# Attention and a 16-entry look-up FFN on one core: look-ups of 1024 columns, placed by two running counts, and six down blocks kept in DRAM

## Chip, cores, metric

One NeuronCore of a Trainium2 chip runs the whole program. The metric is the device time of one execution in microseconds; the median of three runs of the kernel before is 1066.1 us (1065.95 to 1067.05). The engines are named as in the profile: PE (TensorE, matmul), PEld (its weight loads), DVE (VectorE), ACT (ScalarE), POOL (GpSimd) and SP (SyncE, which here only issues DMAs).

## What is computed

All in float32; x has shape (2, 2048, 512), the hidden size of the FFN is 1376, and each FFN weight is an entry of a table of 16.

```python
def attn(x, Wq, Wk, Wv, Wo):          # attention over the 512 features, not over tokens
    q, k, v = x @ Wq, x @ Wk, x @ Wv
    s = softmax(q.T @ k / 4, axis=-1) # 512 x 512, one per batch entry
    return (s @ v.T).T @ Wo
def ffn(x, lut, gate_idx, up_idx, down_idx):
    h = silu(x @ lut[gate_idx].T) * (x @ lut[up_idx].T)   # 1376 wide
    return h @ lut[down_idx].T
x = x + attn(layernorm(x), ...)
x = x + ffn(layernorm(x), ...)
```

## The kernel before, in words

The 4096 tokens are eight chunks of 512. The attention is folded into one 512 x 512 matrix for each batch entry, which is multiplied with the normalized chunks ("y products", 175 to 290 us). The FFN's gate and up products follow (290 to 750 us), then the last 96 of the 1376 hidden rows ("rows", 750 to 798), then the down products in two halves (798 to 931, and 931 to the end).

**Products with fewer multiplications.** Gate, up and down products are done on 2 x 2 blocks with seven products in place of eight (Strassen-Winograd): each needs sums of weight blocks and of activation blocks, named S1 to S4 and T1 to T4, and folds the seven results together. Hidden rows are taken in blocks f of 128 (f = 0 to 10, the last has 96), tokens in pairs p of chunks (p = 0 to 3). A *unit* is one (f, p). From f=2 on, some block products take part in a second level over f and f+1 and over p and p+1: the `Second` objects of_b, of_c and of_d hold sums over both f (tiles lb, lc, ld, made by `sums_left`) and activation sums that are kept in DRAM and loaded again. A unit's role 0 to 3 says where it stands in that square of four. Unit (f, 1) with f even has role 1: right after its first product a1 it multiplies with S2 of lc (`extra0`). Units with f odd take partial results back from DRAM by POOL's DMAs (`add_part` into p1 and u2, `back` into y).

**Order by hand.** The program order of PE, ACT, DVE and SP is the order in which the Python code emits instructions; POOL's queue is ordered by the framework. Each engine works off its queue in order. `Line.run` emits the stages of a unit (a1, c1, a2, c2, b, a3, a4 of the unit before) and calls `between()` after most of them.

**Weights by look-up.** A `Job` makes 512 columns of one weight block (gate, up or down) from int32 indices: `fetch` loads the indices, `cast` (ACT) makes an int16 copy, and `ops` (a generator, all on DVE) makes three masks of single bits and one full-word mask, eight leaves (each chooses between two table entries) and seven merges with copy_predicated. Each `yield` gives the estimated cost of the step emitted. The tiles: `idx` two buffers, results `wg` and `wu` three each. The gate job of block f may start when f < 3 + passed (units of f-3 emitted), the up job when f < 3 + ended (the last a4 of f-3 emitted, one unit later). After an up job, `of_both` makes the sums S1 to S4 of the block (four DVE operations on 256 columns).

`pump(us)` emits look-up steps worth `us`. In gate/up, `between()` first loads or does one thing from a list (sums_left when ready, otherwise one of `todo`), and pumps 0.3 after an operation of `todo`, nothing after sums_left, and `pace[0]` (0.6 to 1.4 by role, 0.75 in down) otherwise. Before a unit, a loop makes sure that its weights are there, and before p = 1 those of f+1 and the lc, lb, ld sums: it emits all steps that are still missing at once.

```python
        while f not in gu or f > 1 and p and not all(o.ready(f | 1) for o in seconds):
            step()
        ...
        while p and sums_of:
            next_sums_left()
```

Down blocks: eleven, of 128 hidden rows x 512. Blocks 0 to 5 lie in `wd`, a tile that is held in SBUF from the start; 6 to 10 are looked up during the first half of down. `down_sums` makes the T sums of the pairs of blocks; `Hidden` loads h from DRAM by SP's queue and makes its S sums, listed in `todo`. The class `LastRows` copies (ACT, lines 1250 and 1251) and sums the weights of block 10; it is set up after the last unit.

Of the kernel before, what the change touches and what calls it, by code (L numbers as in the profile page):

```python
# [62 lines left out]
P = 128  # L63
# [6 lines left out]
def tile_attn_ffn(  # L70
# [39 lines left out]
    wdp = ctx.enter_context(tc.tile_pool(name="wdp", bufs=1))  # L110
# [8 lines left out]
    wd = wdp.tile([P, K1, E], F32, tag="wd", name="wd")  # L119
# [18 lines left out]

    def sub(dest, a, b):
        nc.vector.tensor_tensor(dest, a, b, ALU.subtract)  # L140

    def add(dest, a, b):
        nc.vector.tensor_tensor(dest, a, b, ALU.add)  # L143
# [102 lines left out]
    class Job:  # L246
        def __init__(self, name, rows, cols, load, dest, after, gate):
            self.name, self.rows, self.cols = name, rows, cols
            self.load, self.dest, self.after, self.gate = load, dest, after, gate

        def fetch(self, queue=nc.gpsimd):
            self.idx = gub.tile([P, 512], I32, tag="idx", name=f"idx_{self.name}", bufs=2)[
                : self.rows, : self.cols
            ]
            self.load(queue, self.idx)

        def cast(self):
            self.b3 = self.bits("b3", 2)
            nc.scalar.copy(self.b3, self.idx)

        def bits(self, tag, bufs):
            t = gub.tile([P, 512], I16, tag=tag, name=f"{tag}_{self.name}", bufs=bufs)
            return t[: self.rows, : self.cols]

        def ops(self):

            rows, f, idx, b3 = self.rows, self.cols / 1024, self.idx, self.b3
            vec = nc.vector
            w = self.dest()
            b1, b2 = self.bits("b1", 1), self.bits("b2", 1)  # L270
            vec.tensor_scalar(b1, b3, 2, None, ALU.bitwise_and)
            vec.tensor_scalar(b2, b3, 4, None, ALU.bitwise_and)
            yield 0.2 + 0.54 * f

            vec.tensor_scalar(idx, idx, 31, 31, ALU.logical_shift_left, ALU.arith_shift_right)
            yield 0.1 + 0.55 * f
            vec.tensor_scalar(b3, b3, 8, None, ALU.bitwise_and)
            yield 0.1 + 0.27 * f
            masks = [None, b1, b2, b3]

            def pick(level, at, dest):

                if level == 1:
                    k = at // 2
                    vec.tensor_scalar(  # L285
                        dest.bitcast(I32), idx, lut_x[:rows, k : k + 1],
                        lut_i[:rows, at : at + 1], ALU.bitwise_and, ALU.bitwise_xor,
                    )
                    yield 0.2 + 0.55 * f
                    return  # L290
                yield from pick(level - 1, at, dest)
                half = 1 << (level - 1)
                t = gub.tile(
                    [P, 512], F32, tag="pick", name=f"{self.name}_{level}_{at}", bufs=3
                )[:rows, : self.cols]
                yield from pick(level - 1, at + half, t)
                vec.copy_predicated(dest, masks[level - 1], t)  # L297
                yield 0.1 + 1.17 * f

            yield from pick(4, 0, w)  # L300
            yield from self.after()

# [6 lines left out]
    def gate_job(f):  # L309
        f0, rows = FT[f]  # L310
        n = KB * rows

        def load(queue, idx):
            queue.dma_start(idx, gate_idx[:, KB * f0 : KB * f0 + n])

        def dest():
            t = wgu.tile([P, KB, P], F32, tag="wg", name=f"wg_{f}", bufs=3)
            gw[f] = t.rearrange("p k r -> p (k r)")[:, :n]
            return gw[f]

        def after():
            gw[f] = gw[f].rearrange("p (k r) -> p k r", k=KB)
            yield 0.1

        return Job(f"g{f}", P, n, load, dest, after, lambda: f < 3 + passed[0])

    def up_job(f):
        f0, rows = FT[f]
        n = KB * rows
        up = []  # L330

        def load(queue, idx):
            queue.dma_start(idx, up_idx[:, KB * f0 : KB * f0 + n])

        def dest():
            t = wgu.tile([P, KB, P], F32, tag="wu", name=f"wu_{f}", bufs=3)
            up.append(t.rearrange("p k r -> p (k r)")[:, :n])
            return up[0]

        def after():  # L340
            uw[f] = up[0].rearrange("p (k r) -> p k r", k=KB)
# [4 lines left out]
        def of_both():  # L346
# [4 lines left out]
            for op, d, v, w in (  # L351
                (add, s1, a21, a22), (sub, s2, s1, a11), (sub, a21, a11, a21), (sub, s4, a12, s2)
            ):
                op(d, v, w)
                yield 0.42
            gu[f] = {"11": a11, "12": a12, "S3": a21, "22": a22, "S1": s1, "S2": s2, "S4": s4}

        return Job(f"u{f}", P, n, load, dest, after, lambda: f < 3 + ended[0])

    def down_job(i):  # L360
        f0, rows = FT[i]
        return Job(
            f"wd{i}", rows, E, lambda queue, idx: queue.dma_start(idx, down_idx[f0 : f0 + rows, :]),
            lambda: wd_block(i)[:rows], lambda: iter(()), lambda: i < K1 or wd2,
        )

    wd2 = []

    def wd_block(i):
        return wd[:, i, :] if i < K1 else wd2[0][:, i - K1, :]  # L370


    jobs = [job(f) for f in range(2) for job in (gate_job, up_job)]
    jobs += [down_job(i) for i in range(4)]
    for f in range(2, NFT - 1, 2):
        jobs += [gate_job(f), up_job(f), gate_job(f + 1), up_job(f + 1)]
        jobs += [down_job(i) for i in {6: (4,), 8: (5,)}.get(f, ())]
    jobs += [gate_job(NFT - 1), up_job(NFT - 1), *(down_job(i) for i in range(K1, NFT))]
    assert len(jobs) == 3 * NFT

    def looked_up():

        for i, job in enumerate(jobs):
            while not job.gate():
                yield None
            if i == 0:
                job.cast()
            for k, cost in enumerate(job.ops()):
                yield cost
                if k == 9 and i + 1 < len(jobs):  # L390
                    jobs[i + 1].cast()
            if i + 2 < len(jobs):
                jobs[i + 2].fetch()
# [4 lines left out]
    def step():  # L398
# [6 lines left out]
        return next(lookup, None)  # L405

# [20 lines left out]
    jobs[1].fetch(nc.sync)  # L427
# [337 lines left out]
    def turn(to, t):  # L765

        nc.vector.transpose(to.rearrange("p m (t b) -> p m t b", b=Q), t)
# [124 lines left out]
    class Second:  # L892
# [32 lines left out]
        def ready(self, f):  # L925
            return f in gu if self is of_d else f in gw and len(gw[f].shape) == 3 and f in uw
# [78 lines left out]
    def mm(ps, pairs, first):  # L1005

        for i, (lhsT, rhs) in enumerate(pairs):
            nc.tensor.matmul(  # L1008
# [4 lines left out]
    class GateUp:  # L1013
# [52 lines left out]
        def c2(self):  # L1066
            if self.role is None:
                mm(self.c, self.pairs("22", "T4"), False)
                add(self.u2, self.c, self.u2)
            elif self.role == 0:  # L1070
                of_c.begin(self, "11", "11")
                mm(self.c, of_c.pair(self, "12", "21"), False)
                add(self.u2, of_c.ps, self.u2)
                add(self.u2, self.c, self.u2)
            elif self.role == 1:
                add(self.u2, self.c, self.u2)
                of_c.go_on(self, "S4", "22")
                add(self.u2, of_c.ps, self.u2)
# [30 lines left out]
        def b(self):  # L1109
# [3 lines left out]
            elif self.role == 0:  # L1113
# [3 lines left out]
                add(h0, self.p1, h0)  # L1117
            elif self.role == 1:
                of_b.go_on(self, "S4", "22")
                add(h0, of_b.ps, self.p1)  # L1120
            elif self.role == 2:
                of_b.go_on(self, "22", "T4")
                add(h0, of_b.ps, self.p1)
# [8 lines left out]
        def a3(self):  # L1132
            mm(self.a, self.pairs("S1", "T1"), False)
            self.c22 = self.temp("c22")
            add(self.c22, self.a, self.p7)

        def first(self):
            if self.role == 2:
                add(self.u2, of_c.ps, self.u2)
            if self.role in (2, 3):  # L1140
                add(self.u2, self.c, self.u2)
            nc.vector.tensor_tensor(self.h0, self.h0, self.u2, ALU.mult)
            self.store(self.h0, 2 * self.p)

        def a4(self):
# [3 lines left out]
            elif self.role == 0:  # L1149
# [3 lines left out]
                add(h1, self.a, h1)  # L1153
            elif self.role == 1:
                of_d.go_on(self, "S4", "22")
                nc.scalar.copy(h1, of_d.ps)
                add(h1, self.a, h1)
            else:
                if self.role == 2:
                    mm(self.a, of_d.pair(self, "22", "T4"), False)  # L1160
                    add(self.y, of_d.ps, self.y)
                add(h1, self.a, self.y)
# [6 lines left out]
        def out(self):  # L1169
            nc.vector.tensor_tensor(self.h1, self.h1, self.c22, ALU.mult)  # L1170
            self.store(self.h1, 2 * self.p + 1)

    class Line:
# [5 lines left out]
        def run(self, u, final=False):  # L1179
# [24 lines left out]
            self.between()  # L1204
            if role == 3:
                last_a4()
            u.extra2()
# [24 lines left out]
    class LastRows:  # L1232
# [5 lines left out]
        def __init__(self):  # L1238
            s = [wgu.tile([P, 3, 2, P], F32, tag="s", name=f"last_{i}", bufs=2) for i in range(2)]
            flat = [  # L1240
                t.rearrange("p a b c -> p (a b c)").rearrange("p (k r) -> p k r", k=KB) for t in s
            ]
            self.w, self.v = flat
            t = last_pool.tile([P, KB, 2 * LAST], F32, tag="last", name="last_2")
            self.u = t

        def weights(self):
            f, r = NFT - 1, LAST
            w, v, u = self.w, self.v, self.u
            nc.scalar.copy(w[:, :, :r], gw[f])  # L1250
            nc.scalar.copy(w[:, :, r:], uw[f])  # L1251
# [54 lines left out]
    pace = [1.0]  # L1306
# [4 lines left out]
    def between():  # L1311
# [4 lines left out]
        elif todo:  # L1316
            todo.pop(0)()
            pump(0.3)
        else:
            pump(pace[0])  # L1320
# [216 lines left out]
    def one_by_one(op):  # L1537
        def ops():
            op()
            pump(max(0.0, pace[0] - 0.75))  # L1540
# [6 lines left out]
    line = Line(between)  # L1547
    for (f, p), following in zip(units, units[1:] + [(NFT, 0)]):
        while f not in gu or f > 1 and p and not all(o.ready(f | 1) for o in seconds):
            step()  # L1550
# [8 lines left out]
        if (f, p) == (2, 1):  # L1559
            todo += by_two(in_place)  # L1560
        u = GateUp(f, p)
        pace[0] = {0: 0.85, 1: 1.4, 2: 1.0, 3: 0.6}.get(u.role, 1.07)
# [12 lines left out]
    while uw.get(NFT - 1) is None:  # L1575
        step()
# [6 lines left out]
    last_rows = LastRows()  # L1583
# [20 lines left out]
    pace[0] = 0.75  # L1604
# [86 lines left out]
```

## Time and profile before

| | us |
|---|---|
| median of three runs | 1066.1 |
| the profiled execution, whole | 1067.22 |
| its span, first to last instruction | 1065.4 |
| DVE busy | 837.1 |
| ACT busy | 385.2 |
| POOL busy | 105.7 |
| look-up leaves and merges of 128x512 (L285, L297), mean of one | 0.54 and 0.73 |
| index load on POOL (idx_wd / idx_g), issue to landing, median | 3.1 / 4.0 |

The span is what the trace shows; what lies around it (1.8 us here) is in the run's time only. Busy time is the union of an engine's instructions; the instructions of PE and DVE overlap their neighbours a little, so the mean duration of one is longer than the time from its start to the next start. A wait line reads: engine, what it was about to do, the instruction or DMA whose end released it, us in total, number, longest.

### The profile page before, as it was taken

How to read it: one execution, taken by the hardware profiler on the slowest of the kernel's cores; microseconds unless marked ns; L12 is line 12 of the kernel's file. 1: busy time of each engine (PE TensorE's matmuls, PEld its weight loads, DVE VectorE, ACT ScalarE, POOL GpSimd, SP SyncE). 2: the span in 40 equal slices, each digit the busy share in tenths (PEclk: the TensorE clock that was granted, in tenths of full speed). 3: DMA queues.
4: the chain of work that ended last, by engine and by line, in shares of the span. 5: the costliest groups of instructions: out<-in, count | busy, mean ns of one | idle time of the engine just before them, and what ended most of it. 6: DMA issues, size and time to landing. Idle time of an engine off the chain costs nothing. (4 is left out here: it accounts for less than half of the span.)

```text
span 1065.4 us, 11592 instructions
## 1 busy us (share of the span) xinstructions
PE 1056.6 (99%) x3554; PEld 660.7 (62%) x3554; DVE 837.1 (79%) x1842; ACT 385.2 (36%) x741; POOL 105.7 (10%) x160
## 2 busy tenths in 40 slices
PE   8999999999999999999999999999999999999998
PEld 5668887444444444444444444444898888888887
DVE  7878778889985889899699999964549998656554
ACT  4652532455532234444443444443223222211111
POOL 0000000011110220230041032013000000000000
PEclk9999999999999999999999999999999999999999
DMA  8750314598561366795596679569436675666773
GB/s 345 236 169 11 86 28 99 119 237 222 158 178 50 128 228 197 172 220 183 185 207 198 208 174 225 178 192 195 150 114 230 198 228 177 203 192 211 222 227 119
DMA packets 127710, 189.07 MB, mean 177 GB/s; under 512 B 18832, under 2 KB 59024, under 8 KB 126752
## 3 DMA queue, kind: packets, MB, share of 16 engines
q1 hardware_dynamic: 74528, 100.17, 29.6%
q0 software_dynamic: 15776, 39.92, 17.4%
q10 hardware_dynamic: 37344, 48.24, 13.9%
q8 instruction: 28, 0.46, 0.2%
q14 instruction: 34, 0.28, 0.1%
HBM read 108.60 MB, written 79.69 MB: 177 GB/s over the span
## 5 line engine op out<-in xcount | busy, mean ns | idle before, releaser
L783 PE MATMUL y<-m,nT 128*128 128x512 f32 x256 | 110.2, 592 | 0.0
L783 PEld LDWEIGHTS y<-m,nT 128*128 128x128 f32 x256 | 48.6, 190 | 60.4 <-issue 57.4
L1008 PE MATMUL a_g<-xT_a,s 128*128 128x512 f32 x160 | 75.5, 594 | 0.0
L1008 PE MATMUL a_g<-xb,wg 128*128 128x512 f32 x160 | 75.4, 593 | 0.0
L1008 PE MATMUL c_g<-xb,wu 128*128 128x512 f32 x160 | 75.2, 592 | 0.0
L1008 PE MATMUL a_d<-dT,hs_a 128*128 128x256 f32 x288 | 72.6, 379 | 0.0
L467 PE MATMUL gp<-xn_a 128*128 128x128 f32 (+3 forms) x256 | 70.1, 434 | 1.8 <-DVE xn_a L184 1.5
L467 PEld LDWEIGHTS gp<-xn_a 128*128 128x128 f32 x256 | 43.9, 190 | 28.6 <-issue 15.1
L1008 PEld LDWEIGHTS a_d<-dT,hs_a 128*128 128x128 f32 x288 | 54.5, 189 | 7.7
L297 DVE COPY_PREDICATED wd<-b_wd,wd 128x512 f32<-128x512 int16 (+1 forms) x77 | 56.3, 732 | 1.3
L1008 PE MATMUL a_g<-xT_sq,s 128*128 128x512 f32 x120 | 56.7, 595 | 0.0
L1473 ACT COPY p_d<-a_d 128x256 f32<-128x256 f32 x32 | 11.9, 372 | 120.2 <-PE a_d L1008 120.2
L1008 PEld LDWEIGHTS a_g<-xb,wg 128*128 128x128 f32 x160 | 30.2, 190 | 39.0 <-issue 32.5
L1008 PEld LDWEIGHTS a_g<-xT_a,s 128*128 128x128 f32 x160 | 30.1, 190 | 38.9 <-issue 36.4
L1008 PEld LDWEIGHTS c_g<-xb,wu 128*128 128x128 f32 x160 | 30.4, 190 | 38.3 <-issue 38.0
L143 DVE TENSOR_TENSOR r<-r,p_d 128x256 f32<-128x256 f32 x64 | 26.9, 420 | 28.0 <-ACT p_d L1473 17.4
L285 DVE TENSOR_SCALAR wd<-idx_wd,lut_x,lut_sb 128x512 int32<-128x512 int32 (+1 forms) x88 | 45.9, 539 | 0.0
L1063 ACT COPY u<-a_g 128x512 f32<-128x512 f32 x40 | 23.4, 586 | 61.9 <-PE a_g L1008 59.5
L143 DVE TENSOR_TENSOR u<-c_g,u 128x512 f32<-128x512 f32 x40 | 27.5, 688 | 21.8 <-PE c_g L1008 15.5
L1285 PE MATMUL rows<-last,xb 128*128 128x192 f32 x256 | 41.9, 326 | 1.6 <-ACT last L1251 1.6
L1285 PEld LDWEIGHTS rows<-last,xb 128*128 128x128 f32 x256 | 41.6, 190 | 2.5 <-ACT last L1251 2.5
L143 DVE TENSOR_TENSOR r<-r,a_d 128x256 f32<-128x256 f32 x64 | 26.6, 416 | 20.9 <-PE a_d L1008 20.9
(345 smaller groups left out, 2207.1 us busy)
## 6 DMA issues: line engine op xcount, KB each, us to landing
hd<-h SPq DMA_DIRECT2D x80, 256.0 KB, 3.3
h<-hd SPq DMA_DIRECT2D x40, 512.0 KB, 5.9
nl<-nd SPq DMA_DIRECT2D x32, 256.0 KB, 5.6
xnd<-xn_f ACTq DMA_DIRECT2D x16, 512.0 KB, 5.9
fl<-xnd POOLq DMA_DIRECT2D x32, 256.0 KB, 6.7
xn_back<-xnd SPq DMA_DIRECT2D x32, 256.0 KB, 3.9
rd<-r SPq DMA_DIRECT2D x32, 256.0 KB, 3.0
r<-rd SPq DMA_DIRECT2D x32, 256.0 KB, 4.3
```

Source lines behind the costliest of these rows:

```text
L143: nc.vector.tensor_tensor(dest, a, b, ALU.add)
L285: vec.tensor_scalar(dest.bitcast(I32), idx, lut_x[:rows, k : k + 1], lut_i[:rows, at : at + 1], ALU.bitwise_and, ALU.bitwise_xor,)
L297: vec.copy_predicated(dest, masks[level - 1], t)
L467: nc.tensor.matmul(gp[b][i][:, i * P :], xn[:, i, j % 2, :], xn[:, i:, j % 2, :], start=c % CPB == 0 and j == 0, stop=c % CPB == CPB - 1 a ...
L783: nc.tensor.matmul(ys[k], nTs[k][:, i, :], m[:, i, :], start=(i == 0), stop=(i == KB - 1))
L1008: nc.tensor.matmul(ps, lhsT, rhs, start=first and i == 0, stop=i == len(pairs) - 1, skip_group_check=not first,)
L1063: nc.scalar.copy(self.u2, self.a)
L1285: nc.tensor.matmul(ps[:, jj, :], x[:, j * P : (j + 1) * P], w, start=i == 0, stop=i == len(pairs) - 1,)
L1473: nc.scalar.copy(p1, self.a)
```

## The change

1. A job now makes up to 1024 columns: `pair_job(f)` does gate and up of a block in one tile of three buffers, `down_job(i)` two down blocks. The masks and picks are as wide. The index tile has one buffer; the next job's two index loads are emitted after the last leaf (step LEAVES = 15), its cast after the job's last step.
2. Down blocks 0 to 5 are stored to DRAM (`wdd`, three stores of 512 KB) and loaded again, 1 MB and 0.5 MB, into rooms sq1 and a3 when the last rows begin.
3. A class `Clock` counts, while the code emits, PE's time (matmuls) and DVE's time; folds of a matmul's result (`fold`) set DVE's count to at least PE's. In gate/up, `between()` now calls `fill(lead)`: look-up steps are emitted until DVE's count is `lead` (0.8 us, or -0.5 ahead of a4 in role 3) past PE's. In y products and the attention `pump` stays as it was; in down, `between()` pumps 0.75 whether or not an operation of `todo` went first.
4. The order of jobs: blocks 0, 1, down 0-1, 2-3, block 2, down 4-5, then blocks 3 to 10, then down 6 to 10.
5. The two copies of `LastRows` are emitted ahead of the last gate/up unit. In role 2 the fold of y moves from `a4` to `first`. The gate of a block's job is that of the up job before.

```diff
+    class Clock:
+        pe = dve = 0.0
+        def matmul(self, cols):
+            self.pe += (4 * cols / 2.4 + 5) / 1000
+        def vector(self, cols, of_pe=False):
+            if of_pe:
+                self.dve = max(self.dve, self.pe)
+            self.dve += 0.15 + 1.05 * cols / 1000
...
         def fetch(self, queue=nc.gpsimd):
-            self.idx = gub.tile([P, 512], I32, tag="idx", name=f"idx_{self.name}", bufs=2)[
-                : self.rows, : self.cols
-            ]
-            self.load(queue, self.idx)
+            t = gub.tile([P, 2, 512], I32, tag="idx", name=f"idx_{self.name}", bufs=1)
+            self.idx = self.part(t)
+            for i, of in enumerate(self.loads):
+                queue.dma_start(self.idx[:, i, :], of)
...
-        return Job(f"g{f}", P, n, load, dest, after, lambda: f < 3 + passed[0])
...
+        loads = [idx[:, KB * f0 : KB * f0 + n] for idx in (gate_idx, up_idx)]
+        return Job(f"w{f}", P, n, loads, dest, after, lambda: f < 3 + ended[0])
...
+        def after():
+            if i < K1:
+                nc.sync.dma_start(wdd[:, i : i + k, :], made[0])
+            yield 0.1
...
             for k, cost in enumerate(job.ops()):
                 yield cost
-                if k == 9 and i + 1 < len(jobs):
-                    jobs[i + 1].cast()
-            if i + 2 < len(jobs):
-                jobs[i + 2].fetch()
+                if k == LEAVES and i + 1 < len(jobs):
+                    jobs[i + 1].fetch()
+            if i + 1 < len(jobs):
+                jobs[i + 1].cast()
+                yield 0.9
...
+    def fill(lead):
+        while clock.dve < clock.pe + lead:
+            cost = step()
+            if cost is None:
+                clock.dve = max(clock.dve, clock.pe)
+                return
+            clock.dve += 1.1 * cost
...
-    def between():
+    def between(lead=0.8):
         if to_load:
             to_load.pop(0)()
         if sums_of and sums_of[0][0].ready(sums_of[0][1] | 1):
             next_sums_left()
         elif todo:
             todo.pop(0)()
-            pump(0.3)
+        if pace:
+            pump(pace[0])
         else:
-            pump(pace[0])
+            fill(lead)
...
         while f not in gu or f > 1 and p and not all(o.ready(f | 1) for o in seconds):
-            step()
+            clock.dve += step()
...
+        if (f, p) == (NFT - 2, NPR - 1):
+            while uw.get(NFT - 1) is None:
+                step()
+            last_rows = LastRows()
+            last_rows.copied()
...
+    for q, (tag, n) in enumerate((("sq1", 4), ("a3", 2))):
+        t = room(tag, f"wd_{tag}")[:, :n, :]
+        nc.sync.dma_start(t, wdd[:, 4 * q : 4 * q + n, :])
+        wd1 += [t[:, i, :] for i in range(n)]
```

## The prediction

> **What bounds the kernel now.** I read the page's busy times first, then who TensorE waited for, then the stretches, then the instruction forms, and last the timeline at one place where TensorE waits for the weights' sums.
>
> ```profile
> PE 1056.6 (99%) x3554; PEld 660.7 (62%) x3554; DVE 837.1 (79%) x1842; ACT 385.2 (36%) x741; POOL 105.7 (10%) x160
> ```
> TensorE is busy for 1056.6 of 1065.4 us. Whatever the change does to the other engines can win back only what is missing from the full share.
>
> ```profile
> PE rows L1285 <- ACT last L1251: 1.6, 1, 1.6
> PE ea_s L620 <- ACT a L641: 0.3, 1, 0.3
> PE z_g L1008 <- DVE lc L140: 0.2, 1, 0.2
> PE z_g L1008 <- ACT r_c L958: 0.2, 1, 0.2
> ```
> These are TensorE's waits away from the start (us in total, times, longest). One of 1.6 us is the two copies that begin the last rows; the others are tenths.
>
> ```profile
> 394.00:482.00 88.00, 87.81 (x204) 38.41 (x204) 81.14 (x166) 38.28 (x67) 17.45 (x22) 1.00 0.73 195
> 482.00:566.00 84.00, 83.98 (x195) 36.52 (x194) 71.88 (x135) 35.70 (x63) 16.73 (x22) 1.00 0.71 190
> 657.00:750.00 93.00, 92.03 (x213) 39.95 (x212) 65.33 (x129) 39.55 (x70) 16.81 (x22) 1.00 0.72 192
> 798.00:931.00 133.00, 133.00 (x618) 117.09 (x617) 115.19 (x288) 38.52 (x77) 1.62 (x3) 1.00 0.65 208
> ```
> Columns: stretch, length, then busy time of PE, PEld, DVE, ACT, POOL, the granted clock, DMA share, GB/s. In the gate/up stretches VectorE is busy for 70 to 92%: a second engine close to its limit, in front of whose queue TensorE stands as soon as work for it is bunched. The granted clock is 1.00 throughout.
>
> ```profile
> L297 DVE COPY_PREDICATED g<-b_g,g 128x512 f32<-128x512 int16 x40 | 29.3, 732 | 1.0
> L297 DVE COPY_PREDICATED g<-b_g,g 128x384 f32<-128x384 int16 x4 | 2.3, 587 | 0.1
> L285 DVE TENSOR_SCALAR g<-idx_g,lut_x,lut_sb 128x512 int32<-128x512 int32 x70 | 36.0, 536 | 0.0
> L285 DVE TENSOR_SCALAR g<-idx_g,lut_x,lut_sb 128x384 int32<-128x384 int32 x7 | 3.1, 472 | 0.0
> ```
> A merge goes from 587 to 732 ns over 128 columns, 1.13 ns a column; a leaf from 472 to 536, 0.50. Instructions overlap their neighbours: in the timeline a merge starts at 489.99 and the next instruction at 490.62, so a merge of 512 takes 0.63 us of the engine, a leaf 0.45, a fold from PSUM 0.61, a 256-column sum 0.34, a 128-column sum 0.20. I count with these.
>
> ```profile
> 393.79 0.59 PE L1008 MATMUL a_g<-xb,wg 128*128 128x512 f32 x1
> ...
> 394.23 0.29 DVE L140 TENSOR_TENSOR lc<-lc,wu 128x128 f32<-128x128 f32 x1
> ...
> 394.57 0.70 PE L1008 MATMUL z_g<-T_c_in,lc 128*128 128x512 f32 x1 [0.19 <-DVE lc L140]
> ```
> This is unit (2,1): two matmul pairs of a1, then the product with the second of the lc sums. TensorE would have started at 394.22 (a pair's pass is 0.43 us) and starts at 394.57. The same product of f=4, 6 and 8 does not wait: lc was summed about 10 us earlier.
>
> **The change, part by part.** Times below are on TensorE's own count, the matmuls ahead of an instruction in the queue at 0.86 us per 512 columns; the order is that of the changed program, built and not run. As a test I added up VectorE's queue of the kernel before in this way, each fold starting no earlier than its matmul: from 300 us on it stands up to a few us from the trace, as TensorE's own waits add up, and it gives one late sum, lc of f=2, by 0.1 us where the trace has 0.35.
>
> *Width.* Two look-ups of 512 cost 2 x (8 x 0.45 + 7 x 0.63 + 3 x 0.20 + 0.34) = 17.9 us. At 1024, carried on along the two slopes (merge 1.20, leaf 0.71, the four bit steps 1.6, their 0.20 and 0.34 not quite doubled): 15.7. A merge of 1024 lies between 1.14 (the 1024-column sum's 1.21 us less the overlap) and 1.26 (twice 0.63); I take 1.20. Sixteen jobs save 36 us of VectorE, lying beside TensorE's work: worth nothing directly.
>
> *Where the look-ups stand.* Gate and up are now one job, which starts only when f-3 has ended; before, the gate half could start a unit earlier. The new filler adds look-up steps only while its VectorE count is under TensorE's plus 0.8. After a forced run that count is ahead: w6 is cast at 482.6 and its next steps on the index stand at 499.8. So w5 is not ready when unit (4,1) needs lc, and the loop ahead of the unit empties the rest into VectorE's queue at once. In the changed order, at the end of unit (4,0), VectorE has, after a3: the c22 fold and the h0 product (2 x 0.6, 0.17 behind the matmul), two merges (2.4), four sums of s (1.34), two of lc (0.4), and 0.08 for the last to finish: 5.6. TensorE reaches z_g after a1's two matmuls, 1.7 later, and waits for 3.9. The same run stands ahead of (2,1): 3.9. Ahead of (6,1) and (8,1) the merges are already done: 1.4 + 1.34 + 0.4 + 0.08 - 1.7 = 1.5 each. Sum 10.8; with the 0.25 by which the count was short in the row above and the 0.10 that the restart cost there (the next matmul start was 0.10 late as well), four times, 12.2. In place of f=2's own 0.46: net 11.7. Bounds: 7 (merges at the short price and lc a fold earlier) to 15 (the idle VectorE behind each wait makes a further fold late).
>
> *Down, first half.* The down rounds now always pump 0.75, also where an operation of the list went first (before: 0.3). Per 512 tokens VectorE gets 16 folds of 0.33, 12 sums of 0.33 and 14 x 0.75: 19.8 us against 18.2 of TensorE, until the last look-ups (40 us at these steps) are used up after four rounds. VectorE falls some 5 us back, and the sums of the next hidden tile come after TensorE wants them: 1.4 us at most by the count (at 843). Nought to 4; I take 1.4. The two last index loads stand close to their casts there: 4.4 and 2.5 us of TensorE after VectorE frees the one index buffer, against 0.55 per issue and 3.1 to landing (row idx_wd). ScalarE's copies queue behind the cast; late by up to 1.5, with one stage of 1.3 as cover: 0.4, up to 2 without cover.
>
> *One index buffer.* In gate/up the gap from last leaf to cast is 6.8 to 14.6 us; two issues and a landing of 4.0 take 5.1. Hidden with 1.7 to spare; without it, each late us stops ScalarE's p and u copies, and TensorE behind them. At f=5 the index loads of w8 stand on POOL's queue ahead of u(5,3), which lands 2.4 us after VectorE wants it; folds waiting for TensorE absorb all but 0.5: 0.5, up to 2.4.
>
> *Down blocks through DRAM.* Three stores of 512 KB on SP's queue wait for a last merge that stands at most 3 us back; behind them are loads two blocks of 14 us ahead. Two loads of 1.0 and 0.5 MB follow the three of h at 750.6. At the page's own 128 to 345 GB/s the first MB lands 7 to 20 us after, wanted after 8; VectorE then holds up the rows, which have four banks of 2.6 us: 0, and up to 4 if it lands last.
>
> *Last rows.* The two copies move ahead of the last unit, under its matmuls: -1.9 (1.6 and the slow restart). Other small waits in gate/up, about 2 us in steps of 0.1 to 0.3: 0 to -1.5, I take -0.5. In the y products one transposed tile comes 0.3 late: 0.4.
>
> *Sum.* 11.7 + 1.4 + 0.4 + 0.5 - 1.9 - 0.5 + 0.4 = 12.0 on the span of 1065.4: 1077.4. The profiled execution took 1067.2 in all, 1.8 around the span, 1.1 over the runs' median of 1066.1; on the median: 1078.1, say 1078.
>
> The Trainium skill ("TensorE: Matmul & The Clock Gate", Part 1) has a rule against this change: an idle window of about 3.4 us can halve TensorE's clock until a busy window of that length has passed. No wait in this trace is longer than 1.9, so nothing here shows it; by the page as an estimate the two long waits could cost 1.7 us more each, 1081.5 in all.
>
> **The rivals.** *VectorE's relief is what counts (faster).* 36 us less on an engine busy for up to 92%: lc is in time everywhere, the last rows' wait goes, and part of the small ones: 1066.1 - 1.9 - 1.5 = 1062.7. For it: the DVE column. Against it: the queue order, where lc stands behind the rest of a look-up. It holds if the run ahead of (4,1) ends 3.9 us sooner. 6%, and 3% for ending within 0.2% because only f=2 and part of f=4 wait.
>
> *The index loads decide (slower still).* One buffer, two loads, ScalarE stopped at the cast: with 3 us late at nine jobs of which half reaches TensorE, 13 more: 1091. For it: 1.7 to spare, DMA share 0.7. Against it: landings of 3.1 to 4.0 in the rows. 10%.
>
> *Half of the waits (slower, less).* TensorE's waits push TensorE back, VectorE catches up earlier than counted, part 0 has none: 1066.1 + 7 - 2.4 = 1071. 11%.
>
> **How the numbers follow.** Forecast 70%, 1078. The range takes in the half case and stops below the index loads': 1070.5 to 1084 (the forecast's own bounds, 7 + 0 to 15 + 4, lie about there). What a measurement of this kernel tells from no change is 0.2%, 2.1 us. Faster 6%, same 3%, slower 91%.
>
> **What would show it.** Right: TensorE waiting for DVE lc about four times, two near 4 us and two near 2; the wait for `last` gone; VectorE's busy time down by some 35 us; short waits for h or hs between 800 and 870. Wrong: lc waits under a microsecond, or ACT casts idle on idx loads, or a wait for the reloaded blocks.

## The result and the profile after

| | us |
|---|---|
| after, median of four runs | 1092.45 (1091.31 to 1093.29) |
| before, median beside them | 1066.03 (1065.84 to 1067.05) |
| ratio | 1.0243, interval 1.0231 to 1.0255 |
| profiled execution after: whole, span | 1091.31, 1089.5 |

The change makes the kernel 26.4 us slower. The forecast had the sign, and its 1078 had less than half of the size; the measured time lies outside the range that was given.

The page of the changed kernel, busy time by engine:

```profile
PE 1064.2 (98%) x3554; PEld 661.0 (61%) x3554; DVE 802.0 (74%) x1538; ACT 384.0 (35%) x725; POOL 105.6 (10%) x160
```

VectorE lost 35 us of work, the 36 that were counted from the durations of wider instructions, and the kernel became slower all the same. TensorE, with as many matmuls as before, is "busy" for 7.6 us longer: some of its instructions became slower, in part those that the stretches below show.

TensorE's waits in the changed kernel (us in total, times, longest):

```profile
PE z_g L1050 <- DVE lc L158: 12.0, 4, 4.3
PE c_d L1050 <- DVE h L158: 3.3, 4, 1.3
PE a_g L1050 <- DVE h L158: 2.0, 4, 0.8
PE a_d L1050 <- DVE r L158: 1.8, 3, 0.7
PE idle L487 <- POOL ident masks.py:199: 1.4, 1, 1.4
PE x_g L1050 <- ACT r_b L999: 0.5, 1, 0.5
```

The wait of the rows for `last` is gone. Four waits for lc stand in its place, and lines for h, r and r_b that the list of the kernel before does not have. The stretches (columns as before: stretch, length, busy PE, PEld, DVE, ACT, POOL, granted clock, DMA share, GB/s) of the changed kernel, two around the long waits and one in the first half of down:

```profile
394.00:486.00 92.00, 86.94 (x198) 37.86 (x198) 71.94 (x110) 35.79 (x62) 17.72 (x22) 0.98 0.65 170
486.00:582.00 96.00, 90.88 (x207) 39.27 (x206) 72.91 (x111) 38.28 (x65) 17.33 (x22) 0.98 0.68 183
825.00:892.00 67.00, 61.88 (x279) 51.96 (x278) 64.07 (x135) 17.40 (x34) 1.61 (x3) 1.00 0.56 180
```

and the last of them in the kernel before:

```profile
825.00:892.00 67.00, 67.00 (x312) 58.99 (x311) 61.74 (x152) 19.25 (x38) 1.07 (x2) 1.00 0.65 208
```

Two things are new. In the first two stretches the granted clock is no longer 1.00, and in the third TensorE misses 5 of 67 us while VectorE is at 96%.

To see where the 24.1 us of span (1065.4 to 1089.5) went, I took from the trace of each kernel the times from one matmul's start to the next and summed what exceeds the pass of 0.43 or 0.215 us. This excess is 10.0 us before and 34.1 after, a difference equal to that of the spans, so that nothing else is needed. (The other 2.3 of the 26.4 us lie between runs: the profiled run before was 1.2 above its median, the one after 1.1 below.)

| place | after less before, us | forecast |
|---|---|---|
| z_g for lc (4.49, 4.49, 1.99, 1.93, less 0.46) | +12.4 | +11.7 |
| matmuls at half clock after the two long waits | +3.5 | not in the sum |
| first half of down, 825 to 892 | +7.2 | +1.4 and +0.4 |
| last rows | -1.9 | -1.9 |
| the rest: above all a_g for h at six unit ends, x_g for r_b | +2.8 | -0.5, +0.5 and +0.4 |

The first long wait itself, VectorE's queue at unit (2,1) before TensorE's z_g at 398.43 (timeline of the changed kernel; start, duration, instruction):

```profile
392.43 0.69 DVE L158 TENSOR_TENSOR c<-a_g,p 128x512 f32<-128x512 f32 x1 [0.97 <-PE a_g L1050]
393.04 0.68 DVE L158 TENSOR_TENSOR h<-h,u 128x512 f32<-128x512 f32 x1
393.64 2.62 DVE L328 COPY_PREDICATED w<-b_w,w 128x1024 f32<-128x1024 int16 x2
396.29 0.43 DVE L365 TENSOR_TENSOR s<-w 128x256 f32<-128x256 f32 x1
...
397.77 0.28 DVE L158 TENSOR_TENSOR lc<-w 128x128 f32<-128x128 f32 x1
398.09 0.29 DVE L158 TENSOR_TENSOR lc<-lc,w 128x128 f32<-128x128 f32 x1
```

It is the queue of the forecast, instruction for instruction: fold, product, two merges, four sums, two of lc; 5.95 us from the first start to the last end, where 5.6 was counted from the end of a3. The queue ahead of (4,1), from 491.05 on, has the same instructions.

What follows that wait is the unforeseen part. The stretches around it (columns as above):

```profile
394.90:398.25 3.35, 0.00 (x0) 0.00 (x0) 3.21 (x8) 0.00 (x0) 0.00 (x0) 1.00 0.11 43
398.30:401.65 3.35, 3.22 (x4) 1.52 (x5) 3.28 (x13) 0.58 (x1) 0.00 (x0) 0.50 0.02 5
401.75:405.00 3.25, 3.25 (x9) 1.47 (x8) 1.31 (x3) 1.36 (x3) 0.00 (x0) 1.00 0.22 81
```

TensorE is idle for a whole stretch, then runs at half the clock for 3.41 us, with 4 matmuls in the time of 8, and then at full clock again. The page's row of 40 slices hides this, because a slice of 27 us is only a little under full.

### The profile page after: what moved, and what is told of

The parts are those of the page before. It is cut to its first block, busy times and chain, and to the rows that moved or that the text cites. A ratio compares the mean times of both kernels' runs of the same rounds, so it can differ in the third digit from the quotient of the medians.

```text
span 1089.5 us, 11315 instructions
## 1 busy us (share of the span) xinstructions
PE 1064.2 (98%) x3554; PEld 661.0 (61%) x3554; DVE 802.0 (74%) x1538; ACT 384.0 (35%) x725; POOL 105.6 (10%) x160
## 5 line engine op out<-in xcount | busy, mean ns | idle before, releaser
L328 DVE COPY_PREDICATED w<-b_w,w 128x1024 f32<-128x1024 int16 (+1 forms) x77 | 98.6, 1281 | 1.5
L1050 PE MATMUL a_g<-xb,w 128*128 128x512 f32 x160 | 75.8, 596 | 2.0 <-DVE h L158 2.0
L1050 PE MATMUL c_g<-xb,w 128*128 128x512 f32 x160 | 76.8, 603 | 0.0
L316 DVE TENSOR_SCALAR w<-idx_w,lut_x,lut_sb 128x1024 int32<-128x1024 int32 (+1 forms) x88 | 67.9, 794 | 0.3
L1050 PEld LDWEIGHTS c_g<-xb,w 128*128 128x128 f32 x160 | 31.4, 196 | 40.3 <-issue 40.1
L1050 PEld LDWEIGHTS a_g<-xb,w 128*128 128x128 f32 x160 | 29.9, 190 | 42.3 <-issue 34.2
L1520 ACT COPY p_d<-a_d 128x256 f32<-128x256 f32 x32 | 11.9, 372 | 120.0 <-PE a_d L1050 120.0
L328 DVE COPY_PREDICATED wd<-b_wd,wd 128x1024 f32<-128x1024 int16 (+1 forms) x42 | 50.8, 1209 | 0.4
L158 DVE TENSOR_TENSOR c<-a_g,p 128x512 f32<-128x512 f32 x40 | 27.6, 690 | 30.7 <-PE a_g L1050 29.8
L158 DVE TENSOR_TENSOR u<-c_g,u 128x512 f32<-128x512 f32 x40 | 27.5, 688 | 20.6 <-PE c_g L1050 13.0
```

Of the source, the lines that this page charges most:

```text
L158: nc.vector.tensor_tensor(dest, a, b, op)
L316: vec.tensor_scalar(dest.bitcast(I32), idx, lut_x[:rows, k : k + 1], lut_i[:rows, at : at + 1], ALU.bitwise_and, ALU.bitwise_xor,)
L1050: nc.tensor.matmul(ps, lhsT, rhs, start=first and i == 0, stop=i == len(pairs) - 1, skip_group_check=not first,)
L1520: nc.scalar.copy(p1, self.a)
```

## The experiments

The kernel before took 1066.6, 1066.4, 1066.4 and 1066.5 us beside the four groups (e1 to e4, e5 to e8, e9, e10). All edits are to the changed kernel unless another is named.

**e1: the sums of lc ahead of everything else in the forced run.** Where the loop ahead of a unit with p = 1 empties the look-up into the queue, each set of sums is emitted as soon as its block is ready.

```diff
         while f not in gu or f > 1 and p and not all(o.ready(f | 1) for o in seconds):
-            clock.dve += step()
+            if p and sums_of and sums_of[0][0].ready(sums_of[0][1] | 1):
+                next_sums_left()
+            else:
+                clock.dve += step()
```

> The changed kernel, but in the forced run ahead of unit (f,1) the lc and lb sums are emitted before the four 256-column sums of s. Queue theory with the clock: each of the four waits for lc shrinks by 4 x 0.34 = 1.35 us (4.5, 4.5, 1.9, 1.8 to about 3.1, 3.1, 0.5, 0.5), and as the two long ones then lie under 3.4 us the granted clock stays at 1.00: 5.4 us plus the halved stretches (3.5 in the profiled run, clock 0.997; more in the runs with 0.993) = about 9 to 12 less, 1081 to 1084. Rival, queue alone (the clock falls for another reason, or costs nothing): 5.4 less, 1087. Rival, lc waits for something other than VectorE's queue ahead of it: no change, 1092.

Measured: 1082.5 us (ratio 1.0158, 1.0139 to 1.0176); the four runs 1081.6, 1081.9, 1083.0 and 1087.3, with granted clocks of 1.000, 1.000, 0.998 and 0.995. TensorE's waits for lc:

```profile
PE z_g L1050 <- DVE lc L158: 6.2, 4, 2.9
```

The order within the queue halves the waits (without the restarts z_g starts 3.02, 3.02, 0.43 and 0.36 us late, where it was 4.49, 4.49, 1.89 and 1.82). The time lies in the expected range, but its reason holds only in part: a wait of 3.0 us still halved the clock. The times go with the clock: the same program differs by 5.7 us between runs, the longest with the lowest clock. In the profiled run one of two waits of the same length set off the half clock and the other did not:

```profile
393.85:397.20 3.35, 0.49 (x2) 0.18 (x2) 3.25 (x6) 0.59 (x1) 0.00 (x0) 1.00 0.33 125
397.30:400.60 3.30, 3.30 (x5) 1.24 (x5) 3.16 (x13) 0.59 (x1) 0.00 (x0) 0.50 0.08 28
...
489.40:492.80 3.40, 1.98 (x5) 0.57 (x3) 3.06 (x4) 1.63 (x2) 0.00 (x0) 1.00 0.81 308
492.85:496.20 3.35, 1.96 (x5) 1.01 (x6) 3.21 (x11) 0.58 (x1) 0.00 (x0) 1.00 0.00 2
```

The stretches are laid on a grid of 3.413 us that passes through the fall at 397.26. The first wait fills 85% of one stretch of that grid; the second is cut by a grid line into two stretches in which TensorE is still busy for 58%.

**e2: VectorE's count is kept from running ahead.** Before each unit it is cut to TensorE's plus 1.0. If the forced run begets the next one, because the filler sees a count that is far ahead and emits nothing for a while, this one line must remove the lc waits.

```diff
         assert p in xs
+        clock.dve = min(clock.dve, clock.pe + 1.0)
         if f > 1 and f % 2 == 0 and p == 0:
```

> The changed kernel with one line more: before each gate/up unit VectorE's running count is cut back to at most TensorE's plus 1.0. Theory that the counter, left ahead by the forced run, starves the look-ups that follow and so makes the next forced run: the look-ups of f+1 are done in time, no wait for lc, no fall of the clock: 12.7 + 3.5 to 7 less, 1072 to 1076; what remains above before is the down half. Rival, the 1024-wide look-up gated by the end of f-3 is late whatever the counter says: the waits stay within 1 us of what they were, 1090.

Measured: 1075.9 us (1.0086, 1.007 to 1.0101), clock 1.000. Waits:

```profile
PE a_g L1050 <- DVE h L158: 3.8, 6, 0.7
PE c_d L1050 <- DVE h L158: 3.6, 4, 1.3
PE a_d L1050 <- DVE r L158: 1.8, 3, 0.7
```

No wait for lc is left, and 16.5 us of the median are gone, more than the 12.9 of the waits: the half clock went with them. The waits of a_g for h grew from 2.0 us to 3.8. The look-ups are no narrower and the job order is the same, so it was the placement by the counts.

**e3: the down rounds pump as before.** After an operation of `todo` only 0.3 is pumped in down.

```diff
             todo.pop(0)()
-        if pace:
+            if pace:
+                pump(0.3)
+                return
+        if pace:
             pump(pace[0])
```

> The changed kernel, but in the down half between() pumps 0.3 us after an operation of the list, as before, and 0.75 otherwise. Theory that the added pumping overloads VectorE: the waits for h and r between 825 and 892 (7.3 us in the changed kernel) go, 1085. Rival, the single index buffer (ScalarE's cast waits 2.6 us for the index load of down 8 and 9, VectorE idles 0.9 behind it): they go only in small part, 1090 to 1092.

Measured: 1083.8 us (1.0164, 1.015 to 1.0178). The stretch of down:

```profile
825.00:892.00 67.00, 67.00 (x312) 58.98 (x311) 62.03 (x129) 19.72 (x39) 1.61 (x3) 1.00 0.68 218
```

TensorE is full again, although the index loads, the one buffer and the reloaded blocks are as in the change. The whole down term goes with the 0.45 us of added pumping a stop: 8.7 us of the median, 7.6 of the profiled span. But with less pumping the casts in down also come later behind their loads. The row of these casts in the changed kernel and in e3 (busy, mean ns, then idle time and what ended it):

```profile
L289 ACT CAST b_wd<-idx_wd 128x1024 int16<-128x1024 int32 (+1 forms) x6 | 5.8, 969 | 2.6 <-DMA idx_wd<-in_down_idx_dram 2.6
```

```profile
L289 ACT CAST b_wd<-idx_wd 128x1024 int16<-128x1024 int32 (+1 forms) x6 | 5.8, 970 | 0.0
```

So this run does not separate VectorE's overload from the cast that waits for its load.

**e4: the kernel before, with the two copies for the last rows ahead of the last unit**, and nothing else of the change.

```diff
...
+        if (f, p) == (NFT - 2, NPR - 1):
+            while uw.get(NFT - 1) is None:
+                step()
+            last_rows = LastRows()
+            last_rows.copied()
         u = GateUp(f, p)
...
```

> The kernel before, with only the two copies of the last rows moved ahead of the last gate/up unit. Theory: the wait of 1.6 us with its slow restart goes and nothing takes its place: 1.9 less than before, 1064.2. Rival, another wait (the last folds on VectorE, or the first rows' banks) takes its place: no change, 1066.

Measured: 1064.9 us over eleven runs (0.9984, 0.9975 to 0.9993). The row "rows <- last" is gone from the waits. This is the part of the change that is worth having by itself.

**e5: e2 and e3 together.**

> The changed kernel with both corrections: the counter cut back before each unit, and 0.3 us of pumping after an operation of the list in the down half. Theory that the two losses are independent: 1075.9 less 7.3 to 8.7 = 1067.2 to 1068.6; what is left above the kernel before is the six waits of a_g for VectorE's h at the ends of the units of roles 2 and 3 (4.8 us with their restarts). Rival, VectorE's work only moves and comes due elsewhere: above 1071.

Measured: 1069.0 us (1.0022, 1.0013 to 1.0031), within 0.4 of the expectation. What is left are the six waits of a_g for h, 3.8 us and their restarts; the two parts add up.

**e6: e5, and the filler holds back in front of the folds that free the bank.** In a unit that follows one of role 2 or 3, the filler's lead is -1.0 at the two stops ahead of the `first()` of the unit before.

```diff
+    def lead_at(u, i):
+        return (-1.0,) if isinstance(u, GateUp) and getattr(u, "before", None) in (2, 3) else ()
...
             if last is not None:
                 last.silu()
-            self.between()
+            self.between(*lead_at(u, 0))
...
             u.c1()
-            self.between()
+            self.between(*lead_at(u, 1))
```

> e5 with, in a unit that follows one of role 2 or 3, no look-up step emitted at the two stops ahead of first() unless VectorE's count is 1.0 behind TensorE's (lead -1.0 for 0.8). Theory that those look-up steps stand in front of the folds that free a_g's bank: the six waits go, 4 to 5 less than e5, 1063 to 1064, under the kernel before and level with e4. Rival, the fold chain itself (two of u, h, y, h) is too long: no change against e5.

Measured: 1063.4 us (0.9971, 0.996 to 0.9982), the best kernel of the study. The only wait in gate and up that is left in its list:

```profile
PE z_g L1050 <- ACT r_c L999: 0.5, 1, 0.5
```

So the six waits did come from look-up steps in front of `first()`. Against e4's 1064.9 this is 1.5 us less (1.4 by the ratios), but the two intervals overlap: what 35 us less on VectorE, the new counts and the six blocks in DRAM are worth beyond the moved copies may be nothing, and is 3.5 us at most.

**e7: the change with the old fixed pacing** (0.85, 1.4, 1.0, 0.6 by role, 0.3 in down); wide look-ups, one index buffer, DRAM blocks and moved copies stay.

```diff
...
-        if pace:
+            pump(0.3)
+        else:
             pump(pace[0])
-        else:
-            fill(lead)
...
         u = GateUp(f, p)
+        pace[:] = [{0: 0.85, 1: 1.4, 2: 1.0, 3: 0.6}.get(u.role, 1.07)]
...
```

> The changed kernel with the pacing of the kernel before (fixed shares by role in gate/up, 0.3 after an operation of the list, also in down); look-ups of 1024, one index buffer, the down blocks through DRAM and the moved copies stay. Theory that placement alone lost the time: no waits for lc, none in the down half, the last rows' wait gone: 1064 to 1065. Rival, width and the single index buffer cost something themselves: 1067 or more.

Measured: 1078.4 us (1.0114, 1.0098 to 1.0129). My expectation fell. There is no lc wait and no wait in down, but

```profile
PE a_g L1050 <- DVE h L158: 6.2, 3, 2.1
PE a_g L1050 <- ACT p L1085: 1.5, 4, 0.4
```

and the clock is 0.997. The timeline of VectorE at the first of the three:

```profile
454.95 0.68 DVE L158 TENSOR_TENSOR y<-w_g,y 128x512 f32<-128x512 f32 x1
455.55 1.29 DVE L328 COPY_PREDICATED w<-b_w,w 128x1024 f32<-128x1024 int16 x1
456.73 0.68 DVE L158 TENSOR_TENSOR h<-a_g,y 128x512 f32<-128x512 f32 x1
```

A merge of 1024 columns stands in front of the fold that frees a's bank, and TensorE starts only at 457.46. The stretch 455.05 to 458.45, with TensorE busy for 1.33 of 3.40 us, was followed by 3.41 us of half clock. The third wait, as long as the first two (each start is 2.23 to 2.24 us late), was not followed by half clock. The stretch of the same grid that holds most of it:

```profile
646.20:649.61 3.41, 1.47 (x4) 0.38 (x2) 3.31 (x5) 0.00 (x0) 0.60 (x1) 1.00 1.01 201
```

**e8: the placement without the width.** The kernel before, its 512-column jobs placed by the two counts (here the filler adds each step's cost as it stands, without the 1.1 of the change).

> The kernel before with the counts alone: look-ups of 512 in the old jobs, order, buffers and gates, but placed in gate/up by fill() on the two running counts. Theory that the placement makes the lc sums late and that the wide look-ups even soften it (36 us less of VectorE): several waits for lc of 4 us and more, ended by falls of the clock, and slower than the changed kernel's gate/up part: 1090 to 1115. Rival, the wide jobs make lc late: 1066 to 1070.

Measured: 1131.2 us (1.0606, 1.0586 to 1.0625), worse than expected, clock 0.976:

```profile
PE z_g L1045 <- DVE lc L159: 43.6, 4, 19.3
PE rows L1322 <- ACT last L1288: 5.7, 1, 5.7
```

So the late sums come from the placement, not from the width: here they stand without wide look-ups, and in e7 wide look-ups stand without them. That it is worse than in the changed kernel may come from the narrow steps, which take more of VectorE in all, from the old order of the jobs or from the missing 1.1; no run separates these.

**e9: e7 without the merge in that gap.** In a role-3 unit nothing is pumped between the y fold and the h fold, unless an operation of `todo` stands there.

```diff
             pump(0.3)
-        else:
+        elif lead > 0:
             pump(pace[0])
```

> The kernel of e7_paced (wide look-ups, one index buffer, six down blocks through DRAM, the copies of the last rows moved, the old fixed pacing), but nothing of a look-up is emitted in the one place of a role-3 unit between the y fold and the h fold that frees the bank of a. Theory (e7's loss is a wide merge of some 1.3 us standing in front of that h fold, and the clock falls that these waits set off): the three waits of a_g for h near 455, 551 and 647 go, the granted clock is 1.000, and 12 to 13.5 us of e7's 1078.4 go: 1064.5 to 1066.5. Rival (the width itself bunches VectorE's queue wherever it is emitted, and the steps only move to the next fold): waits of a similar sum appear at another fold, 1072 to 1079, with the clock below 1.000 if one of them passes 2 us.

Measured: 1084.4 us (1.0168, 1.0151 to 1.0185), slower than e7, and outside both expectations.

```profile
PE a_g L1050 <- ACT p L1085: 10.9, 6, 4.0
PE a_g L1050 <- DVE h L158: 3.2, 3, 1.1
```

The three waits for h halved, as the theory has it, but a larger wait appeared some 18 us later, for ScalarE. Its timeline there:

```profile
469.06 0.63 ACT L1167 ACTIVATE h<-h 128x512 f32<-128x512 f32 x1 [3.20 <-DVE h L158]
473.05 1.04 ACT L289 CAST b_w<-idx_w 128x1024 int16<-128x1024 int32 x1 [3.35 <-DMA idx_w<-in_up_idx_dram]
474.00 0.58 ACT L1085 COPY p<-a_g 128x512 f32<-128x512 f32 x1
```

The cast waits 3.35 us for its index load (issued at 466.39, landed 6.6 us later), and behind it stands the copy of p that frees the bank. This is the rival "the index loads decide", which the changed kernel does not show in gate and up: its casts there idle 1.3 us in all, those of e7 8.0 and these 15.2 (11.9 of it for index loads).

**e10: e9 with the cast later.** The pumps skip 3.5 us worth of steps ahead of each cast, so that the two loads have time.

```diff
             if i + 1 < len(jobs):
+                if units_run:
+                    yield 3.5
                 jobs[i + 1].cast()
...
```

> The kernel of e9_pacedgap, with the pumps made to skip 3.5 us worth of look-up steps ahead of the cast of each gate/up job, so that in ScalarE's queue the cast stands some stops later behind its two index loads. In e9 ScalarE idled 3.35 us ahead of a cast whose index loads landed 6.6 us after issue, and the p copy behind it kept TensorE from the bank of a (waits a_g for ACT p 10.9 us in six places, then the clock halved). Theory (with the single index buffer the distance from load to cast is what decides here): ScalarE's idle time for idx_w falls from 11.9 to under 3 us, the waits of a_g for p go but for tenths, the clock is 1.000, and what is left are three waits for h of about 1.1 each: 1067 to 1071. Rival (the wait ahead of the cast only covers VectorE's masks, which still hold b_w, or p is late for another reason): a_g waits for p of over 5 us stay, 1078 or more.

Measured: 1071.1 us (1.0039, 1.0027 to 1.005), clock 1.000: 13 us from the place of the casts (and of the look-up steps, 3.5 us worth of which are held back ahead of each). Waits, and the row of the cast (busy, mean ns, then its idle time and what ended most of it):

```profile
PE a_g L1053 <- DVE h L158: 4.5, 5, 1.1
...
PE a_g L1053 <- ACT p L1088: 1.2, 3, 0.4
```

```profile
L289 ACT CAST b_w<-idx_w 128x1024 int16<-128x1024 int32 (+1 forms) x11 | 11.2, 1021 | 1.7 <-ACT xn_f L264 0.6 <-ACT xn_a L264 0.6 <-ACT r_b L1002 0.5
```

With one index buffer, the distance from load to cast decides under the old pacing, as expected; the time is 0.1 us above the expected range, with five waits for h in place of three.

## Why the forecast was right in kind and wrong in size

**The z_g waits: right.** Four waits, two long and two short, 12.4 us net against 11.7. The reason was right too: the filler's count is ahead after a forced run and it emits too little (e2, e8). VectorE's queue in the trace holds the instructions that were added up, at (2,1) and at (4,1). Three terms of the working are slightly off by its own numbers, without effect on the forecast: four sums of s are 1.36, a round of down is 19.7, and sixteen jobs save 35.2.

**The half clock: weighed, and left out of the sum.** The forecast named it apart from its sum, by the Trainium skill ("TensorE: Matmul & The Clock Gate", Part 1), as an estimate: 1.7 us for each long wait. Measured are 1.7 and 1.8 in the profiled run; the other three runs, whose clocks are lower still (0.993 to 0.995), end 1.1 to 2.0 us later. As no row of before had such a wait, nothing in the case could price it, and the sum had 0 where 3.5 stands.

**The failed step: "Down, first half ... 1.4 us at most by the count ... Nought to 4; I take 1.4", with 0.4 for the casts.** It was 7.2 (7.3 in the texts on e3 and e5), above the 4 and the 2 that bounded the two terms. The overload was stated (19.8 us of VectorE against 18.2 of TensorE a round, for four rounds), but I read its price off as the largest single late sum of the count. Each of the four rounds pays its own wait, 1.6 to 2.1 us with the restarts. The first of each round in TensorE's timeline:

```profile
828.80 0.70 PE L1050 MATMUL c_d<-wd_a,h 128*128 128x256 f32 x2 [0.55 <-DVE h L158]
...
849.00 0.70 PE L1050 MATMUL c_d<-wd_a,h 128*128 128x256 f32 x2 [0.84 <-DVE h L158]
...
869.60 0.70 PE L1050 MATMUL c_d<-wd_a,h 128*128 128x256 f32 x2 [1.25 <-DVE h L158]
...
888.91 0.70 PE L1050 MATMUL c_d<-wd_a,h 128*128 128x256 f32 x2 [0.67 <-DVE h L158]
```

These starts lie 20.2, 20.6 and 19.3 us apart, so a round took about VectorE's time and not TensorE's, while VectorE was busy for 64.07 of 67 us. An engine short by 1.6 us a round for four rounds is 6.4 us late, and that product stood in the text without being taken. On top, VectorE stood still for 0.94 us behind the cast of blocks 8 and 9, whose two loads landed 6.8 to 7.1 us after issue where 3.1 was used; that these 0.94 add to the 6.4 no run of its own shows. ScalarE's timeline there, and the stretch from issue to cast (columns as above):

```profile
842.52 1.04 ACT L289 CAST b_wd<-idx_wd 128x1024 int16<-128x1024 int32 x1 [2.59 <-DMA idx_wd<-in_down_idx_dram]
```

```profile
834.80:842.40 7.60, 7.60 (x37) 6.67 (x37) 7.53 (x16) 0.81 (x3) 1.08 (x2) 1.00 1.02 351
```

The DMA engines had no room in it (share 1.02). The 3.1 was a median; the same loads of the kernel before, between 700 and 931 us, took 2.8 to 7.6, and a term that hangs on one load has to look at the spread.

**The missed term.** "Other small waits ... I take -0.5" was a guess at a gain. In place of it came six waits of a_g for h of 0.1 to 1.0 us at the ends of units of role 2 and 3, and two of x_g for r_b. The six come from look-up steps ahead of `first()` (e6); the two are gone already in e2. The forecast looked at the fold chain only where the long waits were. Its 0.4 for the y products was right (175 to 290 us: +0.4).

**The rest.** The last rows gave 1.9 us as counted, and e4 confirms 1.6 by itself. TensorE has no wait at the reloaded blocks, but VectorE stood still once for the first of them (4.3 us, the line dT <- DMA wd_sq<-wdd of its waits), which landed 10.2 us after its issue; the matmuls of the rows went on without a gap. The index loads did not decide here, though a cast in down did wait for one, which the forecast had named as a sign of being wrong; under another placement they cost 13 us (e9 and e10). VectorE's relief, the faster rival, was worth 1.5 us or so, and by the intervals perhaps nothing, even where nearly every wait that came with it was cured (e6 against e4): TensorE was busy for 99% before, and the missing part was hardly VectorE's.

## What to carry to other kernels

An engine with too much to do in each round can cost the overload times the number of rounds, not just the largest single lag. A filler that places work by a running count must be told what a forced run put ahead of it, or one late block makes the next one late. When a step becomes twice as long, look for every fold that frees a bank with such a step in front of it, and for every blocking cast behind a load, before counting the saving.

## What the hardware showed that I had not expected

TensorE's clock fell to 0.50 for exactly 3.413 us (as the profiler records it) after waits shorter than that: 3.0 us in e1, 2.1 in e7. In e8, whose waits go up to 19.3 us, the falls last two, three or six times 3.413 us. In one execution the falls lie a whole number of 3.413 us apart (398.28 and 497.26 in the changed kernel, 29 times; 95.573 us apart in e7, 28 times), so in these runs the clock is decided at the lines of a fixed grid. By the records, a stretch of that grid in which TensorE, at full clock, was busy for 0 to 39% (1.33 of 3.40 us in e7) was followed by half clock, and those with 43% (1.47 of 3.41 in e7) and 58% (1.98 of 3.40 in e1) were not. So where a wait falls on the grid decides whether it costs 1.7 us more, as the three equal waits of e7 show. This would also explain why runs of one program differ by up to 5.7 us in e1; that last step was not shown, since only one run of each kernel has a trace, and in the four runs of the changed kernel the times do not follow the order of the clocks. The skill's page (the part named above) speaks of an idle window of about 3.4 us, free-running: length and grid agree with these runs, but the window need not be idle throughout.

Not tried: two index buffers for the wide jobs, another order of u(5,3) and the index loads on POOL's queue, and the added pumping in down with earlier loads, which would separate the two parts of the failed term.
